# Pair sums that transpose x itself, with part of the transposes kept in DRAM for the rotation stage

## The chip, the cores and the metric

The kernel runs on one core of a Trainium2 chip. The metric is the device time of one execution in microseconds (us). Three executions of the kernel before took 2761.59 to 2764.78 us, with a median of 2763.41 us.

## The reference, cut to what matters

The input x is (8, 256, 96, 96) in float32: 8 images of 256 channels. Layer 0 normalizes x by groups, makes q, k and v by 1x1 convolutions, takes their 2-D Fourier transforms, lets 8 heads of 32 channels attend to each other over the frequencies, goes back by an inverse transform, takes the absolute value, and adds a 1x1 convolution of it to x. Layer 1 does linear attention on the result.

```python
def _L0_conv_ref(x, w1, b1, w2, b2, w3, b3, w_out, temperature):
    q_f = jnp.fft.fft2(pconv(x, w1, b1), axes=(-2, -1))   # k_f, v_f alike
    q_f = l2_normalize_lastdim(q_f.reshape(b, head, cp, hw))
    attn = jnp.einsum('bhcn,bhdn->bhcd', q_f, k_f) * temperature
    attn = complex(softmax(real(attn)), softmax(imag(attn)))
    out = jnp.einsum('bhcd,bhdn->bhcn', attn, v_f)
    out = jnp.abs(jnp.fft.ifft2(out, axes=(-2, -1)))
    return pconv(out, w_out)
x = x + _L0_conv_ref(_gn(x), ...)
x = x + _L1_conv_ref(_gn(x), ...)      # softplus q and k, linear attention
```

The kernel computes no Fourier transform. The products of q with k over all frequencies follow from sums over pixels of products of channels: of x(p)·x(p), and of x(p)·x(-p), where -p is the pixel mirrored in both directions. With e = x(p)+x(-p) and o = x(p)-x(-p) over half of the pixels, these are two 256x256 matrices, e·e and o·o. The imaginary part of the attention needs x seen through a fixed matrix R over the columns of each row, which the kernel calls the rotation.

## The kernel before, in words

**Layout.** Two SBUF arenas of 128 x 2 x 9216 floats hold x of the running image and of the next. Rows are stored in 12 tiles (NT = 12): tile t holds rows 4t to 4t+3 and their mirror rows (`x_col`, L102), so that 384 columns and their 384 mirrors lie together. Tiles are loaded from t = 11 down to t = 0 (`load_x`, L131).

**Stages of one image b**, as the main loop at L904 makes them:

1. *Attention with rotation* (`weave(attention(b), turns)`, L906): small matrices of the attention, and between them steps of `rotate(b)` (L525). PE's order is the program's here. `yield n` in attention says how many steps of rotate go in at that place; what is left follows in `finish(turns)`. A step (`step`, L539) takes two rows h and h+1: four transposes of x on PE (L550, tile `xr`), one copy by ACT into an SBUF slot of `xT` (L563), and two steps later eight PE passes (L553, tile `y`: four float32 products, each of two passes) of those transposed rows with R (tile `tm`), and two copies by DVE out of PSUM (L558, L559). There are 48 steps. R for six rows at a time is read from DRAM (`load_r`, L533) as a window that slides by one float from partition to partition: 576 pieces of 384 bytes. One column is added by POOL (L536).
2. *Images* (L582): two matmul families, z (L621) and the projection po (L633), on 24 chunks, with ACT, POOL and DVE between them.
3. *Layer 1* (L680): kq (L718), softplus, transposes (L779), kx (L755).
4. *Output* (L835): matmuls o (L863), added into x by DVE (L868) or by ACT and POOL (L871, L872), and the stores of x. In this stage the orders of PE, DVE, POOL and SP are the program's.

**The pair sums of the next image** (`pair_sums(b + 1)`, L323) are woven into stages 2 to 4: one step at a time, as the stages yield, and what is left at the end (`finish(sums)`, L915). There are 37 steps. Before a tile's steps, `even_odd` (L296) makes e and o of four rows into a ring buffer by additions of x with its mirror, on POOL or DVE (L317; the first column of each row by POOL, L318). A step transposes 128 columns of e and o (L350: four PE transposes, tile `eoT`), ACT copies them into one of two `xT` slots (L353), and the eight PE passes of the step before follow (`products`, L328, L331: into the two accumulators `acc`). The statistics of x (L264, DVE) go along. So PE's order in the sums is: transposes of step i, products of step i-1, transposes of step i+1, products of step i.

For image 0 the sums stand alone at the start, while x is loaded. PSUM has five `ps` buffers and three `acc` buffers. The ring has four buffers, and one of them is `own` of layer 1.

Of the kernel before, what the change touches and what calls it, by code (L numbers as in the profile page):

```python
# [47 lines left out]
F32 = mybir.dt.float32  # L50
AF = mybir.ActivationFunctionType
ALU = mybir.AluOpType
# [6 lines left out]
ROWS = 8  # L59
TR = 6  # L60
NZ = 33
NH = 8
# [6 lines left out]
def two_layer_kernel(ctx: ExitStack, tc: tile.TileContext, x, w1t, b1, w2t, b2, w3, b3, wot, temp,  # L69
# [26 lines left out]
    def x_of(b):  # L96
        return arenas[b % 2]
# [25 lines left out]
    def ring_tile(name):  # L123
        return ring.tile([P, 6 * C], F32, tag="ring", name=name)
# [40 lines left out]
    nc.vector.memset(xT[:, :, :, C:C + 2], 1.0)  # L165
    turn = [0, 0]

    def xt_slot(sums=False):

        turn[sums] += 1  # L170
        return xT[:, NX - 2 + turn[1] % 2 if sums else turn[0] % (NX - 2)]

# [6 lines left out]
    nc.scalar.dma_start(out=gri, in_=gmat)  # L179
    half = const.tile([P, 1], F32, name="half")  # L180
    nc.vector.memset(half, 1.0)
    nc.vector.memset(half[0:W], 0.5 ** 0.5)
    hw2 = const.tile([P, 1], F32, name="hw2")
# [44 lines left out]

    rt = dram.tile([H, 2 * W], F32, name="rt")

    def tables():
# [18 lines left out]
        for i in range(2):  # L250
            o = (3 + i) * W
            nc.vector.tensor_copy(t0[:, o:o + 1], r0[:, 0:1])
            nc.vector.tensor_copy(t0[:, o + 1:o + W], r0[:, W - 1:0:-1])
        nc.sync.dma_start(out=rt, in_=t0[:, 3 * W:5 * W])
        load_small()

    def window(h):

        v = rt[h:h + TR, 1:1 + W]
        return bass.AP(v.tensor, v.offset, [[1, W], [2 * W, TR], [1, W]])  # L260

# [31 lines left out]
    def image(t):  # L293
        return t.rearrange("p k (h w) -> p k h w", w=W)

    def even_odd(b, u):  # L296

        assert (b, u % NT) in loaded
        nr = PR if u < NT else 1
        t = ring_tile(f"eo_{b}_{u}").rearrange("p (c k n) -> p c k n", c=2, k=KC)  # L300
        x_t = image(x_of(b))
        rows = [PR * u + i for i in range(nr)]
        if u in (0, NT):
            parts = [(0, 1)] + ([(1, nr)] if nr > 1 else [])
        else:
            parts = [(0, nr)]
        for lo, hi in parts:
            n = hi - lo
            ra = x_col(rows[lo]) // W
            rp = x_col((H - rows[lo]) % H) // W  # L310
            back = slice(rp, rp - n if rp >= n else None, -1)
            for c in range(2):
                eng = nc.vector if u in (0, 1, NT) or (u == NT // 2 - 1 if b else u % 2) else nc.gpsimd
                op = (eng.tensor_add, eng.tensor_sub)[c]
                pop = (nc.gpsimd.tensor_add, nc.gpsimd.tensor_sub)[c]
                d = t[:, c, :, 0:nr * W].rearrange("p k (h w) -> p k h w", w=W)
                op(d[:, :, lo:hi, 1:W], x_t[:, :, ra:ra + n, 1:W], x_t[:, :, back, W - 1:0:-1])  # L317
                pop(d[:, :, lo:hi, 0:1], x_t[:, :, ra:ra + n, 0:1], x_t[:, :, back, 0:1])  # L318
        return t, nr * W

    s0 = {}

    def pair_sums(b):  # L323

        st0 = new_stats(f"st0_{b}")
        acc = [acc_tile(f"acc{c}_{b}") for c in range(2)]

        def products(t, np_, first, last):  # L328
            for c in range(2):
                for m in range(KC):  # L330
                    mm = nc.tensor.matmul(acc[c][:, m * C:m * C + (KC - m) * P], lhsT=t[0:np_, c, m * P:(m + 1) * P],  # L331
                                          rhs=t[0:np_, c, m * P:C], start=(first and m == 0), stop=(last and c == 1),
                                          skip_group_check=True)
                    if first and m:
                        tc.keep_in_program_order(mm)

        pending, first = None, True
        us = [*range(NT - 1, -1, -1), NT]
        ahead = [even_odd(b, us.pop(0))]
        for u in range(NT - 1, -2, -1):  # L340
            u %= NT + 1
            eo, cols = ahead.pop(0)
            for i in range(0, cols, P):
                while i == 0 and us and len(ahead) < (2 if b and u in (NT - 3, NT - 4) else 1):
                    ahead.append(even_odd(b, us.pop(0)))
                np_ = min(P, cols - i)
                pt = ps_tile(f"eoT_{b}_{u}_{i}")
                for c in range(2):
                    for k in range(KC):
                        nc.tensor.transpose(pt[0:np_, c * C + k * P:c * C + (k + 1) * P], eo[:, c, k, i:i + np_], ident)  # L350
                t = xt_slot(True)
                weight = half[0:np_] if u in (0, NT) and i == 0 else 1.0
                nc.scalar.activation(t[0:np_, :, 0:C], pt[0:np_, :].rearrange("p (c n) -> p c n", c=2), AF.Copy,  # L353
                                     scale=weight)
                if pending is not None:
                    products(*pending, first, False)
                    first = False
                pending = (t, np_)
                if u < NT and i:
                    stats_chunk(st0, b, 2 * (NT - 1 - u) + i // P - 1)  # L360
                yield
        s0[b] = st0, acc, products, pending
# [4 lines left out]
    def attention(b):  # L367
# [99 lines left out]

        yield 3

        for m in range(KC):  # L470
# [12 lines left out]
            for j in range(4):  # L483
                s = slice(32 * j, 32 * j + 32)
                nc.vector.tensor_scalar_mul(sbd[s, s], l[s, :], ssum[s, :])
            yield (5, 3)[m]
            pa = ps_tile(f"at_{b}_{m}")
# [37 lines left out]
    def rotate(b):  # L525
# [5 lines left out]
        nc.gpsimd.memset(ys[:, :, 0:1], 0.0)  # L531

        def load_r(h):  # L533
            tm = three.tile([P, TR * (W + 1)], F32, tag="tm", name=f"tm_{b}_{h}")[0:W].rearrange("p (r w) -> p r w", r=TR)
            (nc.scalar if b else nc.sync).dma_start(out=tm[:, :, 0:W], in_=window(h))
            nc.gpsimd.tensor_copy(tm[:, :, W:W + 1], csn[0:W, 2, h:h + TR].unsqueeze(2))  # L536
            return tm

        def step(h, turned):  # L539

            if h is not None:
                pt = ps_tile(f"xr_{b}_{h}")
            if turned is not None:
                g, gt, tm = turned
                pu = ps_tile(f"y_{b}_{g}")
            for r in range(2):
                for k in range(KC):
                    if h is not None and h + r:
                        o = x_col(h + r)
                        nc.tensor.transpose(pt[0:W, r * C + k * P:r * C + (k + 1) * P], x_of(b)[:, k, o:o + W], ident)  # L550
                    if turned is not None and g + r:
                        o = (r * KC + k) * (W + 1)
                        nc.tensor.matmul(pu[:, o:o + W + 1], lhsT=gt[0:W, r, k * P:(k + 1) * P], rhs=tm[:, g % TR + r, :],  # L553
                                         start=True, stop=True)
            if turned is not None:
                src = pu[:, 0:2 * KC * (W + 1)].rearrange("p (r k w) -> p k w r", r=2, k=KC)
                r = 0 if g else 1
                nc.vector.tensor_copy(ys[:, :, g + r:g + 2], src[:, :, W, r:2])  # L558
                nc.vector.tensor_copy(y[:, :, :, g + r:g + 2], src[:, :, W - 1::-1, r:2])  # L559
            if h is not None:  # L560
                xt = xt_slot()
                r = 0 if h else 1
                nc.scalar.copy(xt[0:W, r:2, 0:C], pt[0:W, r * C:2 * C].rearrange("p (r n) -> p r n", n=C))  # L563
                return xt

        tms = [load_r(g) for g in range(0, 3 * TR, TR)]
        pending = []
        for h in range(0, H, 2):
            if h % TR == 0:
                tm = tms.pop(0)  # L570
            if h % TR == 4 and 3 * TR <= h - 4 + 2 * TR < H:
                tms.append(load_r(h - 4 + 2 * TR))
            xt = step(h, pending.pop(0) if len(pending) == 2 else None)
            pending.append((h, xt, tm))
            yield
# [3 lines left out]

    st1s = {}  # L580

    def images(b):  # L582
# [25 lines left out]
        nc.vector.tensor_scalar_mul(tab16, csn[:, 0, :], beta[:, 2:3])  # L608
        nc.vector.tensor_mul(sg[2], sg[2], sg[2])


# [68 lines left out]
    def layer1(b):  # L680
# [72 lines left out]
        def add_kx(i, xt, kT):  # L753
# [3 lines left out]

        extra = [three.tile([P, TR * (W + 1)], F32, tag="tm", name=f"xt{i}_{b}")[:, 0:2 * (C + 2)].rearrange(
            "p (j n) -> p j n", j=2) for i in range(2)]
        for t in extra:  # L760
            nc.gpsimd.memset(t[:, :, C:C + 2], 1.0)
        slots = [*(xT[:, i] for i in range(4)), *extra]
        pend = []
# [202 lines left out]
```

## Time and profile before

| what | us |
|---|---|
| median of three executions | 2763.41 |
| the profiled execution's own time | 2762.53 |
| its span, first to last instruction | 2760.7 |
| attention with rotation, image 1 (415.4 to 489.1) | 73.7 |
| images, image 1, up to the last projections (489.1 to 631) | 142 |
| layer 1, output and the sums of image 2 (631 to 754.9) | 124 |
| first transpose of the rotation, images 0, 1, 2, 3 | 75.1, 415.5, 754.9, 1095.2 |

PE is TensorE's matmul stream and PEld its weight loads, DVE is VectorE, ACT is ScalarE, POOL is GpSimd, SP is the engine that only issues DMAs. A `q` behind a name (SPq, ACTq) is that engine's sequencer issuing a DMA. A group line gives the line of the kernel, engine, operation, what is written from what, shape, count, busy time in us, mean length of one in ns, and the engine's idle time before it. Lengths of PE instructions overlap, since the engine is pipelined: what one instruction costs a busy PE is the distance of the starts, not its length. TensorE's granted clock is 0.993 over the span.

### The profile page before, as it was taken

The page shows a single profiled execution, that of the slowest core. Times are in us where ns is not written, and L with a number is a line of the kernel's source. Part 1 is how long each engine was busy: PE and PEld are TensorE (multiplying, and loading weights), DVE is VectorE, ACT ScalarE, POOL GpSimd, SP SyncE. Part 2 cuts the span into 40 slices and gives each one's busy share as a digit, 9 for nine tenths or more (in the row PEclk, how much of TensorE's full clock was granted, in tenths as well). Part 3 has the DMA queues.
Part 4 walks back from the last instruction along what each step waited for, and adds up shares of the span by engine and source line. Part 5 has one row for each costly group of instructions (what it writes and reads, how often), then busy time and mean ns, then how long its engine had stood idle before and what let it go on. Part 6 is the DMA issues. An engine that isn't in the chain of part 4 may idle for free.

```text
span 2760.7 us, 47785 instructions
## 1 busy us (share of the span) xinstructions
PE 2719.5 (99%) x18348; PEld 1972.5 (71%) x18348; DVE 1958.4 (71%) x4104; ACT 1366.5 (49%) x2098; POOL 841.5 (30%) x939
## 2 busy tenths in 40 slices
PE   8999999999999999999999999999999999999988
PEld 8965679657795677956679566885678856788556
DVE  7588666876668767587675875769766687676776
ACT  3455634556345563355634546345453455544553
POOL 5033340342403423035230351313513135131311
PEclk9999999999999999999999999999999999999997
DMA  5120151201512015120151201521015210251003
GB/s 169 40 65 11 47 184 43 67 9 49 179 43 73 6 47 182 43 69 6 54 179 46 63 6 54 182 54 52 7 53 184 58 46 7 62 178 28 0 7 138
DMA packets 197274, 192.50 MB, mean 70 GB/s; under 512 B 88821, under 2 KB 197049, under 8 KB 197049
## 3 DMA queue, kind: packets, MB, share of 16 engines
q1 hardware_dynamic: 129800, 164.34, 18.8%
q10 hardware_dynamic: 67248, 25.12, 3.6%
q8 instruction: 146, 2.39, 0.4%
q14 instruction: 80, 0.65, 0.1%
HBM read 113.85 MB, written 75.57 MB: 69 GB/s over the span
## 4 chain that ended last, share of the span: by engine, by line
PE 94%; DVE 3%; ACT 2%; DMA 1%; issue 1%; POOL 0%; SPq 0%; POOLq 0%; DVEq 0%; ACTq 0%
PE z L621 21%; PE po L633 18%; PE acc L331 13%; PE y L553 10%; PE xr L550 6%; PE eoT L350 5%; PE xT L779 5%; PE kq L718 5%; PE o L863 4%; PE kx L755 3%; DMA arena<-in_x_dram 1%; PE cw L423 1%; PE kT L770 1%; DVE arena L559 1%; PE mz L511 1%
## 5 line engine op out<-in xcount | busy, mean ns | idle before, releaser
L621 PE MATMUL z<-arena,mz 128*128 128x384 f32 (+2 forms) x2400 | 595.0, 476 | 0.0
L633 PE MATMUL po<-e,wo 128*128 128x384 f32 x1536 | 529.7, 486 | 0.2 <-ACT e L668 0.2
L667 POOL TENSOR_TENSOR e<-e 128x768 f32<-128x768 f32 x192 | 348.2, 1815 | 554.1 <-ACT e L666 554.1
L621 PEld LDWEIGHTS z<-arena,mz 128*128 128x128 f32 (+1 forms) x2400 | 325.6, 163 | 241.4 <-issue 42.4
L553 PE MATMUL y<-tm,xT 96*128 96x97 f32 x3040 | 472.6, 261 | 1.7 <-ACT sd_a L288 0.5
L553 PEld LDWEIGHTS y<-tm,xT 96*128 96x128 f32 x3040 | 457.8, 192 | 12.5 <-issue 4.9
L331 PE MATMUL acc<-xT 128*128 128x256 f32 (+2 forms) x2368 | 440.5, 328 | 3.5 <-ACT xT L353 3.5
L633 PEld LDWEIGHTS po<-e,wo 128*128 128x128 f32 x1536 | 289.4, 190 | 197.7 <-DVE arena L635 1.2
L662 DVE TENSOR_TENSOR e<-z,xT 128x768 f32<-128x768 f32 x384 | 365.7, 953 | 85.2 <-PE z L621 85.2
L264 DVE BATCH_NORM_STATS2 st<-arena 128x6 f32<-128x384 f32 x768 | 406.5, 552 | 13.7 <-DMA arena<-in_x_dram 3.2
L550 PE MATMUL xr<-ident,arena 128*96 128x128 f32 x1520 | 409.2, 275 | 0.0
L331 PEld LDWEIGHTS acc<-xT 128*128 128x128 f32 (+1 forms) x2368 | 380.2, 191 | 37.7 <-ACT xT L353 5.2
L563 ACT COPY xT<-xr 96x512 f32<-96x512 f32 (+1 forms) x384 | 220.2, 578 | 293.8 <-PE xr L550 289.4
L666 ACT ACTIVATE e<-e 128x1536 f32<-128x1536 f32 x192 | 284.6, 1482 | 93.5 <-DVE e L662 92.3
L668 ACT ACTIVATE e<-e 128x768 f32<-128x768 f32 x192 | 161.9, 843 | 334.0 <-POOL e L667 332.9
L317 POOL TENSOR_TENSOR eo<-arena 128x760 f32<-128x760 f32 x136 | 246.1, 1809 | 253.7 <-issue 130.1
L635 DVE TENSOR_TENSOR arena<-arena,po 128x384 f32<-128x384 f32 x384 | 211.1, 551 | 92.6 <-PE po L633 69.5
L353 ACT ACTIVATE xT<-eoT 128x512 f32<-128x512 f32 x280 | 166.6, 598 | 183.9 <-PE eoT L350 182.2
L550 PEld LDWEIGHTS xr<-ident,arena 128*96 128x96 f32 x1520 | 227.2, 150 | 10.3 <-issue 6.9
L559 DVE COPY arena<-y 128x384 f32<-128x384 f32 (+1 forms) x384 | 209.7, 547 | 1.2 <-issue 0.5
L558 DVE COPY ys<-y 128x4 f32<-128x4 f32 (+1 forms) x384 | 62.4, 162 | 199.3 <-PE y L553 195.9
L350 PE MATMUL eoT<-ident,eo 128*128 128x128 f32 (+1 forms) x1184 | 188.1, 280 | 10.4 <-POOL eo L318 10.4
(202 smaller groups left out, 2907.0 us busy)
## 6 DMA issues: line engine op xcount, KB each, us to landing
arena<-in_x_dram SPq DMA_DIRECT2D x184, 384.0 KB
out_dram<-arena SPq DMA_DIRECT2D x184, 384.0 KB
tm<-rt ACTq DMA_DIRECT2D x112, 216.0 KB
tm<-rt SPq DMA_DIRECT2D x16, 216.0 KB
arena<-in_x_dram SPq DMA_DIRECT2D x8, 288.0 KB
out_dram<-arena SPq DMA_DIRECT2D x8, 288.0 KB
wl<-in_w1t_dram SPq DMA_DIRECT2D x8, 256.0 KB
wl<-in_w2t_dram SPq DMA_DIRECT2D x8, 256.0 KB
```

The lines of the kernel that those rows point to most:

```text
L264: nc.vector.bn_stats(out=st[:, k, c, :], in_=x_of(b)[:, k, c * CH:(c + 1) * CH])
L317: op(d[:, :, lo:hi, 1:W], x_t[:, :, ra:ra + n, 1:W], x_t[:, :, back, W - 1:0:-1])
L331: mm = nc.tensor.matmul(acc[c][:, m * C:m * C + (KC - m) * P], lhsT=t[0:np_, c, m * P:(m + 1) * P], rhs=t[0:np_, c, m * P:C], start=(first ...
L350: nc.tensor.transpose(pt[0:np_, c * C + k * P:c * C + (k + 1) * P], eo[:, c, k, i:i + np_], ident)
L550: nc.tensor.transpose(pt[0:W, r * C + k * P:r * C + (k + 1) * P], x_of(b)[:, k, o:o + W], ident)
L553: nc.tensor.matmul(pu[:, o:o + W + 1], lhsT=gt[0:W, r, k * P:(k + 1) * P], rhs=tm[:, g % TR + r, :], start=True, stop=True)
L559: nc.vector.tensor_copy(y[:, :, :, g + r:g + 2], src[:, :, W - 1::-1, r:2])
L621: mm = nc.tensor.matmul(out[:, o:o + n * W], lhsT=columns(mz, k, c, j), rhs=y[:, k, h * W:(h + n) * W], start=(k == 0 and o == 0), stop=(k ...
L633: nc.tensor.matmul(po[:, 0:CH], lhsT=wo[:, k, m * P:(m + 1) * P], rhs=e[:, k, :], start=(k == 0), stop=(k == KC - 1))
L662: nc.vector.tensor_add(e[:, 2 * c:2 * c + 2, :].rearrange("p t (q h) -> p t q h", h=H), pz[:, 0:CH].rearrange("p (q h) -> p q h", h=H).uns ...
L666: nc.scalar.activation(e, e, AF.Square)
L667: nc.gpsimd.tensor_add(e[:, 0:2, :], e[:, 0:2, :], e[:, 2:4, :])
```

## The change

- `pair_sums` no longer forms e and o before the transposes. A step transposes 128 columns of x itself (`front`) and the same number of mirrored columns (`back`, a reversed copy that POOL makes, or ACT for tiles 0 to 4 of images 1 to 7). ACT copies both transposes, scaled by weights `pw`, into the ring buffer (`both`). Then e and o are made of them, on POOL (sum and difference of the two halves of `both`) or on DVE (two scalar_tensor_tensor, one operand of each from PSUM). Column 0 of all rows is gathered apart in `w0`, and rows 0, 48 and `w0` are packed into the last two steps of tile 0 by small copies. There are still 37 steps with four transposes and eight product passes.
- In the steps of tiles 5 to 11 (T0 = 5) ACT's queue also stores both halves of `both` to the DRAM tensor `xtd`: two DMAs of 1 KB rows a step, of 128 rows for j = 0 and 1 and of 127 rows for j = 2. Once an image, `w0` is transposed (two transposes more) and stored in the same way, 28 rows in each of two DMAs.
- `rotate` makes no transposes for the row pairs that are in `xtd` (`spilled`): 27 of 48 steps. It fetches them by SP's queue, three steps ahead, 96 x 2 pieces of 1 KB. Rows above 48 come from the mirrored half, with R turned (`rb`) and the copies to y not reversed. The order of the six-row pieces alternates between pieces that are fetched and pieces that are transposed.
- R with its added column is written to DRAM (`rx`) in image 0 and read from there later, 96 pieces of 2.3 KB a load. POOL's added column (L536) is left to image 0.
- Three yields of attention are larger: 3 becomes 4, and (5, 3) becomes (8, 4). The two buffers of layer 1 that share a pool with `tm` are taken in `images`, since `back` takes the third.

```diff
+T0 = 5
+    rx = dram.tile([H // TR, W, TR, W + 1], F32, name="rx")
+    xtd = dram.tile([2, (H // 2 - PR * T0) * W, C], F32, name="xtd")
+    def turned(c, h, w):
+        return xtd[c, (h - PR * T0) * W + w:]
...
-    def even_odd(b, u):
...
+            ab = sides(t, j)
+            ready = len(ab) == 1
+            front = ab[0][2] if ready else xts[-1][:, j % 3, 0].rearrange("p (k n) -> p k n", k=KC)
+            for p0, n, *v in ab:
+                for c in range(ready, 2):
+                    if v[c] is not None:
+                        (nc.scalar.copy if b and t < T0 else nc.gpsimd.tensor_copy)(
+                            (front, back[:, i % 2])[c][:, :, p0:p0 + n], v[c])
+            return front, xts[-1][:, j % 3]
...
+            if i + 1 < len(steps):
+                ahead = turn_back(i + 1)
+            pt = ps_tile(f"eoT_{b}_{t}_{j}").rearrange("p (c n) -> p c n", c=2)
+            for k in range(KC):
+                nc.tensor.transpose(pt[:, 0, k * P:(k + 1) * P], front[:, k], ident)
+                nc.tensor.transpose(pt[:, 1, k * P:(k + 1) * P], back[:, i % 2, k], ident)
+            nc.scalar.activation(both, pt, AF.Copy, scale=pw[:, j:j + 1])
+            if t >= T0:
+                n = P - j // 2
                 for c in range(2):
+                    nc.scalar.dma_start(out=turned(c, PR * t, 1 + P * j)[0:n], in_=both[0:n, c])
+            eo = sum_slot()[:, :, 0:C]
+            if j % 2 if t >= T0 or not b else t or j < 3:
+                nc.gpsimd.tensor_add(eo[:, 0], both[:, 0], both[:, 1])
+                nc.gpsimd.tensor_sub(eo[:, 1], both[:, 0], both[:, 1])
+            else:
+                for c, op in enumerate((ALU.add, ALU.subtract)):
+                    nc.vector.scalar_tensor_tensor(eo[:, c], in0=pt[:, 0], scalar=pw[:, j:j + 1], in1=both[:, 1],
+                                                   op0=ALU.mult, op1=op)
             if pending is not None:
                 products(*pending, first, False)
...
-        yield 3
+        yield 4
...
-            yield (5, 3)[m]
+            yield (8, 4)[m]
...
+        def spilled(h):
+            return PR * T0 <= h < H - PR * T0 and h != H // 2
...
+            if b:
+                nc.scalar.dma_start(out=tm, in_=rx[h // TR])
+                return tm
...
+        pieces = [TR * i for i in (15, 4, 0, 5, 3, 14, 6, 8, 7, 1, 9, 12, 10, 2, 11, 13)]
+        order = [h + r for h in pieces for r in range(0, TR, 2)]
...
+                nc.sync.dma_start(out=xts[i][0:W, :, 0:C], in_=rows.rearrange("(r w) n -> w r n", w=W))
...
+            step(None if spilled(h) else h, pending.pop(0) if len(pending) == 2 else None, xts[i])
+            pending.append((h, xts.pop(i), tm))
+            fetch(i + 3)
             yield
```

## The prediction on record

> **What bounds the kernel now.** I read the page's head and chain of waits first: they say which engine ends last.
>
> ```profile
> span 2760.7 us, 47785 instructions
> ...
> PE 2719.5 (99%) x18348; PEld 1972.5 (71%) x18348; DVE 1958.4 (71%) x4104; ACT 1366.5 (49%) x2098; POOL 841.5 (30%) x939
> ...
> PE 94%; DVE 3%; ACT 2%; DMA 1%; issue 1%; POOL 0%; SPq 0%; POOLq 0%; DVEq 0%; ACTq 0%
> ```
>
> PE is the chain for 94% of the span. So a PE instruction removed is time gained, at its price in the order of PE, and work added to the others is free until PE waits for it. The mean lengths of the groups (261 ns for `y`, 275 ns for `xr`) overlap and can't be used as prices. The timeline at the end of a rotation can. Its DVE rows (start, length) mark each step:
>
> ```profile
> 484.71 0.16 DVE L558 COPY ys<-y 128x4 f32<-128x4 f32 x1 [0.61 <-PE y L553]
> ...
> 485.94 0.16 DVE L558 COPY ys<-y 128x4 f32<-128x4 f32 x1 [0.61 <-PE y L553]
> ...
> 487.18 0.17 DVE L558 COPY ys<-y 128x4 f32<-128x4 f32 x1 [0.61 <-PE y L553]
> ...
> 488.07 0.16 DVE L558 COPY ys<-y 128x4 f32<-128x4 f32 x1 [0.27 <-PE y L553]
> 488.15 0.55 DVE L559 COPY arena<-y 128x384 f32<-128x384 f32 x1
> 488.96 0.17 DVE L558 COPY ys<-y 128x4 f32<-128x4 f32 x1 [0.27 <-PE y L553]
> ```
>
> Steps with four transposes and eight `y` passes are 1.23 us apart (484.71, 485.94, 487.18). The last two have eight passes alone and are 0.89 apart. Beside a transpose a pass costs less than in a row of its own kind, so a step loses 0.34 us with its transposes, less than the four would seem to cost. DVE needs 0.63 to 0.72 us a step (0.08 from start to start, then 0.55), under 0.89.
>
> The sums alone, after the last output matmul:
>
> ```profile
> 743.10 0.60 PE L350 MATMUL eoT<-ident,eo 128*128 128x128 f32 x4
> 743.54 1.47 PE L331 MATMUL acc<-xT 128*128 128x256 f32 x8
> 744.85 0.60 PE L350 MATMUL eoT<-ident,eo 128*128 128x128 f32 x4
> ```
>
> A step is 1.75 us here; woven with output it is 2.76.
>
> **The change part by part.**
>
> *Rotation, removed:* 27 of 48 steps lose their transposes: 27 x 8 x 0.34 = 73.4 us of PE, all on the chain. *Added:* two transposes an image for `w0`, at 0.11 (0.89/8): 1.8 us.
>
> *Rotation, moved:* the rows come by SP's queue, 192 packets of 1 KB. Queue q1 spent 18.8% of 16 engines' span on 129,800 packets, 64 ns each at 1266 B, so 1 KB is about 52 ns: 12 packets an engine, 0.62 us a fetch, under a step's 0.89. It is issued five steps (4.5 to 6 us) before its use, with no store left on SP in this stage. I take 0; if that cover is gone PE waits at each fetch, at most the fetch again, 0.6 us x 216 = 130. R comes in 96 large pieces instead of 576 small ones and POOL's L536 goes; neither is on the chain: 0.
>
> *Attention:* steps that fill its waits shrink from 1.23 to 1.08 on average ((21 x 1.23 + 27 x 0.89)/48); the enlarged yields put 36 instead of 31 in, so the cover is 39 us where it was 38. 0.3 us an image for unlucky places: 2.4.
>
> *Sums.* Four transposes and eight passes stay, so PE's own time stays. What is new is the wait. Before, a step's products needed transposes and one ACT copy (0.60, L353). Now e and o are made after that copy. On POOL: 128x384 takes 1000 ns (L653) and 128x768 1815 (L667), so 128x256 is estimated at 0.73, twice 1.46. On DVE: 128x384 is 551 ns (L745), 128x256 about 0.42, twice 0.84. From the start of the transposes: 0.70 to ACT's start, 0.60, then 1.46 and some 0.1 is 2.9 us with POOL, 2.2 with DVE. PE comes to these products after one step and the next transposes, 1.75 + 0.44 = 2.19. DVE's is even, POOL's is 0.7 late; since the next transposes are already out, a late step gives the next one slack and half is lost: 0.35 a POOL step. Where other work is woven in (2.76 a step) it is hidden; POOL then has L872 1.00 + 1.46 + small copies 0.13 = 2.6 of 2.76 us, just enough.
>
> Back to back are, for images 1 to 7: the seven steps after the last output matmul. Five use POOL, 1.75 us; the last two need 17 small copies on ACT, 0.2 us each by the smallest ACT rows (128x2, 0.20), which push their copies about 1.0 late: 2.8 x 7 = 19.6. About five at the start, three of them by POOL: 1.0 x 7 = 7. Image 0: 12 POOL steps, 4.2, and the small copies on POOL, 3.8: 8. DVE is full in 661 to 679 (17.96 of 18.0 us); two products more there, 0.5 x 7 = 3.5.
>
> The waits on `eoT` before products bound these from below by 0 (before, PE waited for nothing here), from above by 0.35 on all 296 steps, 104 us.
>
> *Stores on ACT's queue:* 44 DMAs an image. ACT has room:
>
> ```profile
> 612.00:716.00 104.00, 102.84 (x889) 73.25 (x888) 65.58 (x127) 55.63 (x101) 34.05 (x37) 1.00 0.15 43
> ```
>
> (PE, PEld, DVE, ACT, POOL busy in the stretch of the stored tiles): 48 us free, and an issue of ACT's takes 0.3 to 0.5 us: 13 to 22 us. Behind a store that waits stand ACT's copy of the next step, kq and xT evictions, and so PE. For 128 rows I take 0. The 14 stores of 127 rows an image are the unknown. If spread over 16 engines like the 96 and 128 rows of every large DMA here, a store is 8 packets an engine, 0.4 us. If on one engine, 127 x 52 ns = 6.6 us. The trace has no row count that 16 doesn't fit evenly but 8 and 1: q1's 129,800 packets are 121,956 of data by the shapes and 7,844 closing ones, 16 for each of 510 DMAs less 316 = 32 x 8 + 4 x 15, so an 8-row DMA uses 8 engines and a 1-row DMA one. That fits "rows split evenly" as well as "all that there are". I take the nearest row, 128: 0, and keep the other end as a rival.
>
> The Trainium skill, "DMA: Bandwidth & Descriptors", section on why a DMA increments its semaphore by 16, speaks against the change: the number of engines is the largest up to 16 that divides the slowest dimension, and 127 partitions go to 1. The packet counts agree for 1, 8, 96 and 128 rows; no run here shows 127. By that rule the sum would be the rival's below, not the forecast's.
>
> **Sum:** -73.4 + 1.8 + 2.4 + 19.6 + 7 + 8 + 3.5 = -31. The profiled execution took 2762.53 us, 1.8 over its span; 2762.5 - 31 = 2731.4. The median is 0.9 above the profiled execution: 2732.
>
> **Rivals.**
>
> 1. *Slower: the 127-row stores hold ACT.* A queue that issues stores is held when packets pile up:
>
> ```profile
> 714.13 2.56 SPq L882 DMA_DIRECT2D out_dram<-arena  x4
> ...
> 716.79 0.98 SPq L135 DMA_DIRECT2D arena<-in_x_dram  x1
> ```
>
> A lone issue is 0.38; the last of these takes 0.98, its own 16 packets an engine (16 x 61 ns). Two stores of 127 packets on one engine drain in 13.2 us and would hold ACT 7 to 12 of them, once a tile, 56 times. PE goes on for some 3 us on free PSUM buffers. With 10 held: 7 x 56 = 390, so 2732 + 390 = 3120; if ACT isn't held and only landings and loads are late, 1 to 2.5 us a tile: 2790 to 2870. It decides when a 127-row store uses fewer than about four engines, 1.7 us a store. Against it: every large DMA in this trace spreads over 16.
> 2. *POOL's lateness everywhere:* the 0.35 is paid on all steps, -73 + 1.8 + 104 + 2.4: 2797. For it: POOL is 94% full in output. Against it: woven steps leave 2.76.
> 3. *It doesn't do what it says:* the fetches come late and PE waits in their place, giving back most of 73: 2760 to 2790. Against it: the five steps.
> 4. *All waits hidden:* -73 + 2 = 2692. For it: PE waits 10.4 us in all for `eoT` now.
>
> **Numbers.** Forecast (2705 to 2757) 0.44; rival 4 0.05; rival 1 0.38, 2 0.05, 3 0.04; within 0.2% of before (5.5 us, about what a measurement of this kernel can tell from no change) 0.04. Faster 0.49, same 0.04, slower 0.47. Cases of both signs hold most of the chance: the likeliest one's own range is 2705 to 2757; the range that leaves out about 2 in 10 (below rival 4, and the upper third of rival 1) is 2692 to 3120.
>
> **What would show it.** Rotation: 656 `xr` transposes instead of 1520, and `y` copies of DVE 0.89 apart in fetched steps. Fetches: no PE idle ended by a DMA into `xT`. Sums: PE idle before the products, ended by POOL, 0.35 a step, in the last seven steps of an image. Stores: ACT's issues of 0.3 to 0.5 us each; issues of several us, and ACT copies late behind them, mean rival 1, and the forecast is wrong by hundreds of us.

## The result, and the profile after

Four executions of the changed kernel took 3049.82 to 3057.21 us, median 3051.88, beside 2762.95 for the kernel before on the same chip: a ratio of 1.105, 95% interval 1.103 to 1.107. The change is 289 us slower; the forecast was 2732. The head of the page, the granted clock and the chain by engine:

```profile
span 3048.0 us, 47359 instructions
...
PE 2782.4 (91%) x17500; PEld 1984.9 (65%) x17500; DVE 1988.1 (65%) x4285; ACT 1310.0 (43%) x2107; POOL 855.7 (28%) x1216
...
PEclk7789998999989999899999999899998999989997
...
PE 75%; DMA 10%; ACTq 4%; ACT 4%; DVE 4%; issue 3%; POOL 1%; POOLq 0%; SPq 0%; DVEq 0%
```

PE has 848 matmuls fewer, as intended, and is the chain for 75% of the span instead of 94%. DMA has 10% and ACT's queue 4%. The row PEclk has 7s and 8s all along; in the page of the kernel before it is

```profile
PEclk9999999999999999999999999999999999999997
```

ACT's rows in image 0 (start, length) show what the chain waits for; L403 is the store:

```profile
66.62 0.69 ACT L399 ACTIVATE xt<-eoT,pw 128x512 f32<-128x512 f32 x1 [5.48 <-PE eoT L398]
67.33 5.69 ACTq L403 DMA_DIRECT2D xtd<-xt  x2
73.07 1.26 ACT L399 ACTIVATE xt<-eoT,pw 128x512 f32<-128x512 f32 x2 [5.77 <-DMA xtd<-xt]
73.79 8.61 ACTq L403 DMA_DIRECT2D xtd<-xt  x4
```

A row of x2 or x4 covers several issues and what lies between them. Narrower windows take the two rows apart:

```profile
67.33 5.20 ACTq L403 DMA_DIRECT2D xtd<-xt  x1
...
73.79 1.20 ACTq L403 DMA_DIRECT2D xtd<-xt  x3
...
82.15 0.24 ACTq L403 DMA_DIRECT2D xtd<-xt  x1
```

So ACT stands still in two ways. One issue alone is held for 5.20 us. And between the third and the fourth of the other row ACT waits for 7.2 us: by the trace's semaphore events an earlier store lands at 82.13, and the fourth is issued at 82.15. The copy of the next step comes behind both. In the whole span 78 of the 352 issues into `xtd` take over 1 us, 226 us together, the longest 8.74; waits for landings before such issues come to some 110 us. PE's longest waits name the same place from the other side (total, times, longest):

```profile
PE acc L329 <- POOL xT L406: 64.5, 35, 8.6
PE o L964 <- ACT po L972: 55.2, 7, 8.6
PE eoT L397 <- ACT xt L424: 36.0, 7, 5.6
...
PE y L650 <- DMA xT<-xtd: 1.5, 2, 0.9
```

POOL is only the last link in the first line: a wait of 8.6 us is no POOL addition, but one that could not start. The third is the copy of the `w0` transposes, with its store behind it (L427). The fourth is all that PE waits for the fetches.

One table by stage for the kernels that matter below. "Idle" is the sum of PE gaps over 0.1 us and the time before its first matmul; "clock" is the sum of (1 - granted clock) x width over windows of 2 us, so much PE time was lost to the half clock (the last stage always has some 19 to 22). Times are of the profiled execution; that of e8 is its slowest, 2764.62 us, where its median is 2752.10.

| kernel | start | rotation x8 | images x8 | layer 1 + output x7 | the last | span | idle | clock |
|---|---|---|---|---|---|---|---|---|
| before | 75.1 | 587.7 | 1114.0 | 885.7 | 98.2 | 2760.7 | 33 | 19 |
| changed, 127 rows | 152.6 | 557.3 | 1112.1 | 1124.8 | 101.2 | 3048.0 | 257 | 163 |
| 128 rows (e1) | 85.1 | 549.8 | 1112.1 | 935.2 | 101.2 | 2783.5 | 76 | 50 |
| no stores, no fetches (e2) | 81.9 | 589.5 | 1112.1 | 908.3 | 98.2 | 2789.9 | 54 | 19 |
| e1, yields, late w0 (e8) | 88.8 | 527.7 | 1112.1 | 933.7 | 100.6 | 2762.8 | 68 | 41 |
| e8, products two behind (e10) | 81.2 | 514.2 | 1112.1 | 921.8 | 98.1 | 2727.5 | 45 | 31 |

Of the 287 us, 77 come at the start (image 0's sums alone), 239 in layer 1 and output; the rotation gave 30 back. Idle rose by 224 and clock by 145, PE's own work fell by the forecast's 72: 224 + 145 - 72 = 297, so the account closes within 10 us.

### The profile page after: what moved, and what is told of

Same layout as the page of the kernel before. It is cut to its first block, busy times and chain, and to the rows that moved or that the text cites. A ratio compares the mean times of both kernels' runs of the same rounds, so it can differ in the third digit from the quotient of the medians.

```text
span 3048.0 us, 47359 instructions
## 1 busy us (share of the span) xinstructions
PE 2782.4 (91%) x17500; PEld 1984.9 (65%) x17500; DVE 1988.1 (65%) x4285; ACT 1310.0 (43%) x2107; POOL 855.7 (28%) x1216
## 4 chain that ended last, share of the span: by engine, by line
PE 75%; DMA 10%; ACTq 4%; ACT 4%; DVE 4%; issue 3%; POOL 1%; POOLq 0%; SPq 0%; DVEq 0%
PE z L726 19%; PE po L738 16%; PE y L650 11%; DMA xtd<-xt 8%; PE acc L329 8%; PE kq L823 4%; ACTq L403 4%; PE o L964 3%; PE xr L647 2%; PE xT L880 2%; ACT xt L399 2%; PE eoT L397 2%; PE kx L860 1%; PE eoT L398 1%; DMA arena<-in_x_dram 1%
## 5 line engine op out<-in xcount | busy, mean ns | idle before, releaser
L329 PE MATMUL acc<-xT 128*128 128x256 f32 (+1 forms) x2368 | 493.1, 354 | 85.6 <-POOL xT L406 64.5
L329 PEld LDWEIGHTS acc<-xT 128*128 128x128 f32 x2368 | 413.5, 206 | 143.2 <-POOL xT L406 76.4
L650 PE MATMUL y<-tm,xT 96*128 96x97 f32 x3040 | 424.3, 277 | 2.6 <-DMA xT<-xtd 1.5
L399 ACT ACTIVATE xt<-eoT,pw 128x512 f32<-128x512 f32 x296 | 202.8, 686 | 300.7 <-PE eoT L398 148.2
L969 DVE TENSOR_TENSOR arena<-arena,o 128x384 f32<-128x384 f32 x288 | 142.6, 550 | 189.4 <-PE o L964 189.3
L410 DVE SCALAR_TENSOR_TENSOR xT<-eoT,pw,xt 128x256 f32<-128x256 f32 x258 | 113.3, 478 | 222.8 <-ACT xt L399 211.8
L659 ACT COPY xT<-xr 96x512 f32<-96x512 f32 (+1 forms) x168 | 95.4, 572 | 310.1 <-PE xr L647 300.2
L383 POOL COPY back<-arena 128x256 f32<-128x256 f32 (+1 forms) x188 | 86.1, 462 | 400.1 <-PE eoT L398 400.1
L397 PE MATMUL eoT<-ident,arena 128*128 128x128 f32 x560 | 153.2, 298 | 46.8 <-ACT xt L424 36.0
L973 POOL TENSOR_TENSOR arena<-arena,po 128x384 f32<-128x384 f32 x96 | 96.1, 1001 | 309.2 <-ACT po L972 305.5
```

Of the source, the lines that this page charges most:

```text
L397: nc.tensor.transpose(pt[:, 0, k * P:(k + 1) * P], front[:, k], ident)
L399: nc.scalar.activation(both, pt, AF.Copy, scale=pw[:, j:j + 1])
L650: nc.tensor.matmul(pu[:, o:o + W + 1], lhsT=gt[0:W, 1 - r if back else r, k * P:(k + 1) * P], rhs=tm[:, g % TR + r, :], start=True, stop=True)
```

## Experiments

Three theories. A: the 127-row stores use one DMA engine and hold the queue that issues them. B: the sums' new wait for e and o costs the time. C: any store on ACT's queue does. Rival 3 of the prediction (late fetches) fell at once, by the 1.5 us above.

**e1_all128: 128 rows in every store.** `xtd` gets one row more, and the extra row is overwritten by the w0 store.

```diff
-    xtd = dram.tile([2, (H // 2 - PR * T0) * W, C], F32, name="xtd")
+    xtd = dram.tile([2, (H // 2 - PR * T0) * W + 1, C], F32, name="xtd")
-                n = P - j // 2
+                n = P
```

> The changed kernel with one thing different: the store of j = 2 takes 128 rows instead of 127 (the extra row is column 0 of the next row, which the w0 store overwrites later, so the work and the output are the same). Theory A (the 127-row stores run on one DMA engine, as the 5792 closing packets of the changed kernel say, and hold ACT's queue): the sum on record without that term, 2732 us, within 2705 to 2757, and no issue of a store on ACT's queue over 2 us. Theory B (the sums' new wait on POOL and DVE before the products is what costs): no change, 3040 to 3060 us. Theory C (any store by ACT's queue holds ACT, whatever its rows): also 3040 to 3060 us, with the long issues still there.

Measured: 2785.89 us, ratio 1.0087 (1.0065 to 1.0109). One row more in 112 DMAs takes away 266 of the 289 us. Issues into `xtd` over 1 us fall from 78 to 4, and an issue now takes 0.39 on average (137.5 us for 352). The line of the stores (count: shortest, median, longest in ns), in the changed kernel and here:

```profile
L403 ACTq DMA_DIRECT2D xtd<-xt x336: 243/443/8742, 8.4 to 2684.0; - x168
...
L403 ACTq DMA_DIRECT2D xtd<-xt x336: 326/332/1571, 8.4 to 2433.5; - x168
```

B and C fall as the main cause; A is shown. But A's number, 2732, is missed by 54.

The packet records say how. The closing packets are those of 4 bytes; by the counts here a DMA has one on each engine that takes part. Queue q10 (ACT's) has 5792 closing packets of 4 bytes in the changed kernel and 7472 with 128 rows, 1680 = 112 x 15 more: a 128-row store closes 16 engines, a 127-row store one. The rest fits the same count: 341 DMAs x 16, 16 w0 stores of 28 rows x 14, 112 x 1 make 5792. The median packet of 1 KB takes 46 ns, so a 127-row store is estimated at 5.8 us on its engine and a pair at 11.7.

**e2_nospill: the sums' new form alone.** No stores, no w0 transposes, all 48 steps transposed.

```diff
         def spilled(h):
-            return PR * T0 <= h < H - PR * T0 and h != H // 2
+            return False
```

> The changed kernel without any stores to xtd, without the w0 transposes, and with all 48 steps of the rotation transposing x as before; the sums stay in their new form. No part of the result is left out. Theory A: only the sums' own terms of the record are left, 2762.5 + 19.6 + 7 + 8 + 3.5 = 2801 us (2795 to 2810). Theory B (the sums' wait costs the 290 us): 3050 us plus the transposes that come back in the rotation, 45 to 73 us, so 3095 to 3125 us. Theory C (stores by ACT): as theory A, 2801 us.

Measured: 2791.12 us, ratio 1.0093 (1.0078 to 1.0109). The sums cost 25.5 us (29.2 in the profiled executions: 6.8 at the start, 22.6 in layer 1 and output), a little under the 38 on record. PE's waits in this version are those the record described:

```profile
PE acc L329 <- POOL xT L402: 13.2, 24, 0.9
PE acc L329 <- DVE xT L406: 11.4, 8, 1.6
```

**e3_sp127: the 127-row stores by SP's queue.**

```diff
-                    nc.scalar.dma_start(out=turned(c, PR * t, 1 + P * j)[0:n], in_=both[0:n, c])
+                    (nc.sync if j == 2 else nc.scalar).dma_start(out=turned(c, PR * t, 1 + P * j)[0:n], in_=both[0:n, c])
```

> The changed kernel with the 127-row stores issued by SP's queue instead of ACT's; their rows and their engine are the same. If what costs is that ACT is held behind them (theory A, first form): ACT's waits go and 2790 to 2870 us are left, the price on record for late landings and loads alone. If what costs is the one clogged DMA engine, which every load of x and every store of the output also needs (theory A, second form): 3000 to 3060 us, with SP's queue held instead of ACT's. Theory B: 3040 to 3060 us.

Measured: 2932.74 us, ratio 1.0609 (1.0594 to 1.0625), between the two forms. Now SP is held, and ACT's issues are all under 1 us:

```profile
718.72 5.25 SPq L403 DMA_DIRECT2D xtd<-xt  x1
...
L403 ACTq DMA_DIRECT2D xtd<-xt x224: 326/333/807, 8.4 to 2568.1; - x112
L403 SPq DMA_DIRECT2D xtd<-xt x112: 216/767/5976, 31.9 to 2570.8; - x112
```

Layer 1 with output falls from 1124.8 to 1018.3 us, but the start stays at 147.0. It isn't the loads of x that the sums wait for there, though they share SP's queue: all 25 are issued before the first of these stores. ACT's copies wait for stores to land:

```profile
0.74 30.44 SPq L139 DMA_DIRECT2D arena<-in_x_dram  x25
31.88 7.64 SPq L403 DMA_DIRECT2D xtd<-xt  x3
...
44.81 0.69 ACT L399 ACTIVATE xt<-eoT,pw 128x512 f32<-128x512 f32 x1 [12.38 <-DMA xtd<-xt]
...
129.95 0.69 ACT L399 ACTIVATE xt<-eoT,pw 128x512 f32<-128x512 f32 x1 [21.65 <-DMA xtd<-xt]
```

PE's idle between matmuls `o` even grows, from 55.2 to 80.2 us; the experiments with `w0` below say why. So whichever queue issues such a store is held, and who stands behind it or waits for its landing sets the price.

**e4_cut122 and e7_cut124: the dose.** The store is cut into 122 + 5, or 124 + 3 rows.

```diff
-                    nc.scalar.dma_start(out=turned(c, PR * t, 1 + P * j)[0:n], in_=both[0:n, c])
+                    for lo, hi in [(0, 122), (122, n)] if j == 2 else [(0, n)]:
+                        nc.scalar.dma_start(out=turned(c, PR * t, 1 + P * j)[lo:hi], in_=both[lo:hi, c])
```

> The changed kernel with each 127-row store cut in two, of 122 rows and of 5 rows. Theory A with the rule that the number of engines is the largest up to 16 that divides the rows: 122 rows go to 2 engines, 61 packets each instead of 127 on one, and 5 rows to 5; the two stores of a tile then drain in about 6 us instead of 13, and half or less of the excess stays, 2760 to 2890 us. Theory A with a rule that every count which is no multiple of 16 falls on one engine: 3040 to 3070 us, as now. Theory B: 3040 to 3060 us.

> The changed kernel with each 127-row store cut into 124 and 3 rows. By the rule of the largest divisor up to 16, 124 rows go to 4 engines, 31 packets each, where 127 rows put 127 on one. The record names four engines as the point from which the stores decide: then this is near the 128-row version, 2785 to 2810 us. If the cost goes with the packets on the fullest engine alone, on a line through 122 rows (61 packets, 109 us over the 128-row version): 31 packets give 30 to 55 us over it, 2815 to 2840. If the cost came from having more DMAs on ACT's queue, which this version shares with the cut at 122: 2895 us as there.

Measured: 2894.72 us (ratio 1.0464, 1.0449 to 1.0480) and 2861.57 us (1.0347, 1.0332 to 1.0362). Both have 6464 closing packets, 112 x (2 + 5) and 112 x (4 + 3) in place of 112 x 1. That fits the largest divisor of the rows up to 16 as the number of engines, and not one engine for every count that is no multiple of 16. Over the 128-row version 127, 122 and 124 rows cost 266, 109 and 76 us. Both cuts are worse than expected (2760 to 2890, and at most 2840 by the packets); most issues are short now (27 us in those over 1 us), yet PE still idles 51.7 us between matmuls `o` with 124 rows.

**e6_late_w0 and e9_cut124_late: the wait of the w0 store.** It writes into the same tensor, so ACT waits for the stores to land before it issues it. In the changed kernel:

```profile
842.30 0.37 ACT L424 COPY xt<-w0T 77x256 f32<-77x256 f32 x1 [7.50 <-issue]
849.05 5.61 ACTq L427 DMA_DIRECT2D xtd<-xt  x2
854.70 0.48 ACT L972 COPY po<-o 128x384 f32<-128x384 f32 x1 [12.03 <-DMA xtd<-xt]
```

ACT does nothing for 12.03 us, near the 11.7 of a pair, and the copy of `o` comes behind. The edit moves the block, to the 127-row version (e6) and to the cut at 124 (e9):

```diff
-            if (t, j) == (T0, 2):
+            if (t, j) == (T0 - 2, 2):
```

> The changed kernel, 127-row stores and all, with the transposes and the store of w0 made six steps of the sums later, in tile 3 instead of tile 5; its work is the same. The w0 store writes into the same DRAM tensor as the 127-row stores and ACT waits for their landing before it issues it. If that wait is one of the ways in which the slow stores reach PE: the PE idle between two matmuls o (55.2 us) and before the transposes behind w0 (36.0 us), 91 us in all with some clock behind it, goes and 2915 to 2965 us are left. If only the held issues of the stores themselves cost: 3040 to 3055 us.

> The cut into 124 and 3 rows (2862 us, 75 over the 128-row version) with the transposes and the store of w0 six steps later. In the cut version PE idles 51.7 us between matmuls o in the step where ACT waits for the landing of the stores before it issues w0's. If that wait is all that 4 engines still cost: the 52 us of idle and the clock behind it go, 2780 to 2800 us, and four engines are the point at which the stores themselves no longer decide, as the record says. If the packets on the fullest engine cost otherwise: 2835 to 2862 us.

Measured: e6 3004.70 us (ratio 1.0855, 1.0825 to 1.0885), 47 less; e9 2813.04 us (1.0175, 1.0160 to 1.0191), 49 less. Neither lies in a range that was expected: 2915 to 2965 for e6, 2780 to 2800 or 2835 to 2862 for e9. The wait for landing is a second way in which slow stores reach PE. In e6 the two gaps shrink by 64 us and PE's idle in all by 40, since others grow (before the products 103.5 us instead of 85.6). What four engines still cost beyond it is 37 us over 2776 (the 128-row version less the 10 us that a late w0 saves with 128 rows, below; no run has that pair alone): four engines are not yet free.

**e5_cover and e8_both: what is left of the 54 us.** In the 128-row version the rotation gained 38 us, not the forecast's 69. Windows of 3 us at image 1 (length; busy us and instructions of PE, PEld, DVE, ACT, POOL; granted clock; DMA share and GB/s):

```profile
427.00:430.00 3.00, 2.18 (x20) 2.01 (x19) 2.10 (x8) 2.13 (x3) 0.00 (x0) 1.00 0.00 0
430.00:433.00 3.00, 2.72 (x12) 1.31 (x13) 1.47 (x7) 0.00 (x0) 0.00 (x0) 0.54 0.23 75
433.00:436.00 3.00, 3.00 (x17) 3.00 (x17) 1.87 (x7) 0.27 (x1) 0.00 (x0) 0.50 0.25 69
436.00:439.00 3.00, 3.00 (x19) 2.46 (x19) 2.28 (x8) 0.95 (x2) 0.00 (x0) 0.82 0.23 70
```

PE idles 1.1 us before the matmuls `qkm`, and then its clock is 0.5 for 7 us. It has two such idles an image from image 1 on:

```profile
PE at L555 <- DVE scr L552: 8.7, 7, 1.2
PE qkm L459 <- issue: 7.7, 7, 1.1
```

The edit gives attention's two waits four more steps of the rotation. It is made to the 128-row version; e8 has the late w0 store as well:

```diff
-        yield 2
+        yield 4
-            yield (8, 4)[m]
+            yield (10, 4)[m]
```

> The 128-row version with two yields of the attention enlarged, 2 to 4 before the matmuls qkm and 8 to 10 before the first matmul at: four more steps of the rotation lie in the two places where PE idles 1.1 and 1.24 us an image. Nothing else changes. In the 128-row version the rotation stage takes 549.8 us in all, with 18.8 us of PE idle and 22.2 us lost to a granted clock of 0.5. Theory D (the half clock is set off by the two idle places): both go, the stage falls to 512 to 520 us and the kernel from 2786 to about 2750. Theory E (the half clock comes from the lighter stage itself or from the DMA traffic of the fetches): only the idle goes, about 2770. If the steps that are put there leave later waits uncovered: 2786 or more.

> The 128-row version with both edits: the two enlarged yields of the attention and the w0 store six steps later. Over the version with the yields alone this tells what the w0 store costs when the stores land quickly: PE idles 6.5 us between matmuls o there, and that stretch is 1.5 to 1.9 us an image longer than without stores, so 5 to 13 us less than the version with the yields alone, about 2742 us. If the w0 store costs only through slow landings: the same as the version with the yields alone, within 3 us.

Measured: e5 2762.39 us (ratio 0.9995, 0.9982 to 1.0009), e8 2752.10 us (0.9957, 0.9943 to 0.9970). The same place in e5:

```profile
440.00:443.00 3.00, 3.00 (x29) 3.00 (x28) 2.03 (x7) 2.13 (x3) 0.00 (x0) 1.00 0.00 0
443.00:446.00 3.00, 3.00 (x29) 2.22 (x29) 2.64 (x12) 0.37 (x1) 0.00 (x0) 1.00 0.65 182
```

No idle and no half clock here, though the fetches go on: theory D. Images 1 to 7 take 63.9 to 64.3 us, from 67.6 to 74.2 in e1. The expected 2750 was missed by 12 in the median and by 21 in the profiled execution. There image 0's rotation went from 66.6 to 76.1, with an idle of 1.9 us and 21 us at half clock, and layer 1 with output took 9 us more than in e1, since the idle before `o` (9.3 us for 6.5) was followed by half clock five times instead of twice. The late w0 saves 10.3 us between the medians, with quick stores. Executions of these two lie 17 to 19 us apart, where the kernel before has 3 to 8: in e5 they go with the granted clock, 2771.5 us at 0.983 and 2758.4 at 0.988.

**e10_depth2 and e11_all: the sums' lateness.** Both are e8 with the products two steps behind where a third slot is free (`deep[0]` is true in image 0 and from the output stage on, so two steps may be due):

```diff
-        turn[0] += 1
-        return xT[:, NX - 2 + turn[0] % 2]
+        i = min((4, 5, 3) if deep[0] else (4, 5), key=turn.index)
+        turn.remove(i)
+        turn.append(i)
+        return xT[:, i]
...
-            if pending is not None:
-                products(*pending, first, False)
+            while len(due) > deep[0]:
+                products(*due.pop(0), first, False)
                 first = False
-            pending = (eo, P)
+            due.append((eo, P))
```

> The version with 128 rows, enlarged yields and the late w0 store (2752 us), in which the sums run their products two steps behind the transposes instead of one, in image 0 and during output, where a third slot for e and o is free. The work is the same. If the sums' own term is the lateness of e and o behind ACT's copy (the 0.35 to 1 us a step of the record; PE idles 29.3 us before products here, and the sums alone cost 29 us in the version without stores): the start falls from 88.8 to about 82 us, the seven stages of layer 1 and output from 934 to 905 to 915, and 2715 to 2732 us are left. If POOL, ACT or DVE are simply too full in these steps, the delay comes back in the next step: 2745 to 2755 us.

> As the version with products two steps behind, but the enlarged yields are left out in image 0, where R still comes by SP's queue in small pieces and the rotation takes 78.5 us with the enlarged yields and 66.6 without. If its wait is for R, which the earlier steps ask for sooner: 9 to 12 us less than the version with products two steps behind. If the 12 us were image 0's late stores or fetches: no difference.

Measured: e10 2731.71 us (ratio 0.9879, 0.9859 to 0.9899): 20 us less, and faster than the kernel before by 1.2%. The waits that e2 showed, here (lines are two to six further down):

```profile
PE acc L331 <- POOL xT L408: 6.5, 7, 0.9
...
PE acc L331 <- DVE xT L412: 5.0, 8, 1.6
```

PE's idle before the products falls from 33.9 us in e8 to 11.6. The start falls to 81.2 us, as expected, and layer 1 with output to 921.8, where 905 to 915 was expected. So it was mostly latency, not too little throughput. e11, which takes the enlarged yields back in image 0, is 2732.12 us (0.9879, 0.9865 to 0.9892): no difference, since e10's image 0 rotates in 66.3 us with them. My explanation by late loads of R fell; why it took 76 to 79 us in e5 and e8 stays open.

**e12_127: 127 rows in the mended version.** One edit against e10: `n = P - j // 2` again, with the shorter `xtd`.

> The version with 128 rows, enlarged yields, late w0 store and products two steps behind (2732 us), with the stores of j = 2 back at 127 rows and nothing else changed: what 112 stores on one DMA engine cost with every other fault of the change mended. With late w0 alone the 127 rows cost 219 us more than 128 rows (3005 against 2786). If the held queue and the late loads of x are a price of their own: 200 to 220 us, 2932 to 2955 us. If the products two steps behind take up a hold of ACT of 3 to 4 us a tile, as two steps of 1.75 us would: half of it or less, 2790 to 2845 us.

Measured: 2957.15 us, ratio 1.0707 (1.0678 to 1.0735): 225 us over e10, so 4.0 us for each of 56 pairs, beside the 219 of the expectation. Two steps of slack take up none of it.

## Why the prediction was wrong, point by point

- **The step that failed: "I take the nearest row, 128: 0"** for the 14 stores of 127 rows an image. The runs put 266 us there (225 with all else mended). Without it the change would still be slower than the kernel before, by 20 us (e1): the terms below that were mis-sized make 54 us, more than the forecast gain of 31. Rows 128 and 127 are neighbours in length and far apart in the engines they use. The trace of before held two counts that spoke for a divisor or a minimum alike (8 and 1), and I chose by nearness between ends of 0 and 390. The Trainium skill, "DMA: Bandwidth & Descriptors", section on why a DMA increments its semaphore by 16, gave one engine. The 5792 closing packets agree, and the counts of the other runs fit 14 engines for 28 rows, two for 122 and four for 124.
- **Rival 1, at a chance of 0.38, was the mechanism, its price too high.** It priced 7 us a tile, 3120; measured are 4.0 to 4.75 a tile, 3052. Stage by stage it is 3.9 a tile where other work is woven in ((1124.8 - 935.2) / 49) and 9.6 at the start, where none is ((152.6 - 85.1) / 7). The rival let PE go on for 3 us a tile; I read the difference as PE going on longer where other work stands beside the sums. Its main form had the held issue and not the waits for landing, of which w0's alone is 47 us (e6). Its form "ACT isn't held", 2790 to 2870, priced landings at 1 to 2.5 us a tile; e3 (2933) is 2.6 a tile over the 128-row version. Its point of decision, four engines, was near: 37 us are left there.
- **Rotation, -73.4 + 1.8: right.** y copies of the changed kernel are 0.89 apart in fetched steps and 1.23 in others:

```profile
587.71 0.16 DVE L655 COPY ys<-y 128x4 f32<-128x4 f32 x1 [0.61 <-PE y L650]
...
588.94 0.16 DVE L655 COPY ys<-y 128x4 f32<-128x4 f32 x1 [0.61 <-PE y L650]
...
589.84 0.17 DVE L655 COPY ys<-y 128x4 f32<-128x4 f32 x1 [0.27 <-PE y L650]
...
590.73 0.16 DVE L655 COPY ys<-y 128x4 f32<-128x4 f32 x1 [0.27 <-PE y L650]
```

  There are 656 `xr` transposes, as forecast. With the waits covered (e5) a rotation takes 64 us instead of 73.4, 9.4 less, where 73.4/8 = 9.2 were forecast.
- **Attention, 2.4: wrong in size.** I compared total cover and not each wait, and the sum was off too: the mean step is 1.04 by its own figures, not 1.08, so the cover was 37 us for 38, not 39. Two waits of 1.1 to 1.24 us came bare, 16 us of idle in all, and 22 us of half clock behind them: the 128-row version's rotations are 37 us over 8 x 64.1.
- **Sums, 38: near.** 25 to 29 in e2. By place, over the kernel before: the last steps of an image 12.9 us for 19.6; the steps from `den` to the first `o`, which I take for "the start", 9.3 for 7; layer 1, where PE idles 1.57 us an image behind DVE, 5.7 for 3.5; image 0 6.8 for 8; and the steps between the first and the last `o` gave back 5.5 that the forecast didn't have. e10 took 20 back.
- **128-row stores and w0 on ACT, 0 and 1.8: wrong in size.** Layer 1 and output cost 27 us more with stores than without (935.2 for 908.3); 10 of it is the w0 store's wait. Its transposes were priced at 0.22 us an image; the step that holds them is 3.33 us long, from `o` to `o`, instead of 2.75, so 0.58. The rest I read as ACT's 138 us of issue time pushing its copies, which no run took apart.
- **Fetches, 0: right.**
- The terms close to a few us, each read from one execution: 2732 + 35 (attention) + 25 (stores and w0) + 3 (the last stage) - 9 (sums) = 2786, the 128-row version; + 266 = 3052. That e10 lands on 2732 is chance: it has the stores' cost and not the sums'.

## What to carry to other kernels

Before a DMA's price is taken from one with nearly as many rows, count its closing packets or its divisors: here one row more was worth 266 us, and padding the tensor by a row took that cost away. A store is priced by what stands behind it on its queue, and by who waits for its landing, which here was another store into the same tensor. When PE work is taken out of a stage that covers another's waits, check each wait against the steps that are left beside it, not their sum.

## What the runs showed of the hardware that was not expected

- An idle PE can cost more than its idle time. In the 128-row version each of the ten stretches at clock 0.5 between the start and the last stage follows 1.1 to 1.24 us of idle (in one gap or two within 4.5 us) by at most 3.4 us, and lasts 3.4 to 10.2 us. Such an idle doesn't always set one off: of the 14 in the rotations eight were followed by one, and in e2 seven idles of 1.57 us in layer 1 by none. A shorter one can: in e11 one of 0.50 us in a rotation was followed by 3.4 us at 0.5, while those of 0.43 to 0.6 us in image 0's rotation of the 128-row version by none. In the changed kernel 145 us more of clock were lost than in the kernel before. The Trainium skill, "TensorE: Matmul & The Clock Gate", section on how the gate's oscillation bites in real kernels, states that gaps over about 3.4 us must be avoided; here 1.1 us was enough in some places, and the measurement decides.
- e10 has six such stretches with no idle over 0.05 us in the 5.9 us before them, each behind the matmuls `rec` and `o`, which use 32 of 128 rows. Each comes 5.9 to 7.0 us after an idle of 0.92 us before the products, one of seven; in the 128-row version the same seven idles were followed by none. What sets them off was not tried.
- Both queues that were tried are held by stores that pile up on one engine: a single issue takes up to 8.74 us on ACT's (the changed kernel) and up to 5.98 us on SP's (e3), where the median issue of the 128-row version takes 0.33.
